# A four-layer graph network on one core: the last graph's output by halves, a closer spacing of the last graphs, and a longer hold of VectorE behind powers

## The chip, the core and the metric

One NeuronCore of a Trainium2 chip runs the whole kernel in one launch. Its engines are TensorE (PE in the profile; PEld is its weight load), VectorE (DVE), ScalarE (ACT), GpSimd (POOL) and SyncE (SP, which here issues every DMA). They run side by side and wait for each other on semaphores; each works through its own list in order. The metric is the device time of one execution in microseconds (us); lower is better.

## What is computed

There are 32 independent graphs of 512 nodes with 256 features each, all in float32. A graph passes through four layers, and each layer ends in x = layernorm(x + layer(x, adj)):

```python
# layer 0
h = (1.0 + eps) * x + adj @ x
y = relu(h @ W1 + b1) @ W2 + b2                      # 256 -> 512 -> 256
# layer 1
h = adj @ (x @ W.T + b)
y = where(h > 0, h, alpha * h)
# layer 2
h = layer_norm(x, gamma, beta)
y = x + relu((adj @ h) @ W_rel + b_rel + h @ W_root)
# layer 3
agg = eps * x + adj @ x
h = silu(rmsnorm(agg @ W1 + b1) * w)                 # 256 -> 1024
y = h @ W2 + b2                                      # 1024 -> 256
```

## The kernel before, in words

**Products.** Every large product is cut into 2 x 2 blocks and done with seven block products in place of eight (`seven`, line 648), at the price of sums of blocks on VectorE (`left_sums`, `right_sums`). A graph takes 218 matmuls, 106 with 256 columns and 112 with 128. Each leaves two records in the trace[...]. The results come out of PSUM through VectorE additions (`add` in `take` and `put`) or ScalarE copies.

**Norms.** Tokens stand on partitions: a graph's x is a tile of 128 partitions by 4 chunks by 256 features. `Norm` (line 893) gets the sum and the sum of squares of each chunk from ScalarE (`half`, two chunks at a time), scales them on VectorE, takes the power -1/2 on GpSimd (`inv_sqrt`, an instruction of 128 x 4, or of 128 x 8 in layer 1, where two scales are needed), and then scales each chunk (`scaled`, line 927) on VectorE or on ScalarE, whichever the planner finds free. The first and the last graph (`alone`, line 512) use `NormOnVector` at the end of layer 3, with `bn_stats` on VectorE in place of ScalarE's sums, and they spread the RMS norm of layer 3 over tokens with four flips by TensorE (`everywhere`, line 981, operand `ident`), where the other graphs send it through DRAM by DMA. The RMS norm of layer 3 has a power of 32 x 16.

**How the order is made.** Nothing is issued while the layers are traced. Each operation goes into a list (`Plan.do`, `Plan.move`) with the engines it may run on and a cost per engine. `order` (line 351) then plays a list schedule: at each step it takes the engine that can start first, and on it the ready operation of the lowest rank; the operations are issued in the order in which they were picked. Rank is a due time: the graph's number times `period` (42), plus the place of the operation in its graph, counted back from the matmul that needs it (`needs`, line 321). The last few graphs are spaced by `last` instead of `period`: with FLIGHT = 5 (line 496) `final` is graph 27 (line 353), and graphs 28 to 31 follow at 20 or at 12. `best` (line 345) tries each entry of RULES (line 92) as (period, pace, last, near) and keeps the one whose order ends first in the planner's own count; here it is the first entry, 20. Up to five graphs are in work at once, and the buffers (36 rooms in SBUF, 11 small tiles, 8 PSUM banks) limit what may start.

**The hold.** A GpSimd power reads SBUF next to VectorE. The planner marks VectorE operations with two tensor operands in SBUF (TWO_OPERANDS, line 79) with `port`. When VectorE has computed the input of a power, `port["vector"]` is set to the end of that operation plus PORT (line 434): until then the planner starts no two-operand operation on VectorE, but others may pass. Where VectorE would stand idle for that reason, the idle time is written out as memsets of a small tile `pause`, one for every 0.11 of the planner's time (lines 1166 to 1168).

**The trace's lines.** All compute instructions are issued from line 295 and all DMAs from line 313, so lines tell little, and tiles and shapes have to be read: `room` is any large tile, `few` a small one, `ps` a PSUM bank, `L_gnn_*` and `A` are weights and their block sums. `ps<-L_gnn_W,room` and `ps<-A,room` with 128 columns are the last products of layers 0 and 3 (`dense_add`, line 847).

Of the kernel before, what the change touches and what calls it, by code (L numbers as in the profile page):

```python
# [11 lines left out]
AF = mybir.ActivationFunctionType  # L12
ALU = mybir.AluOpType
# [3 lines left out]
LN_EPS = 1e-5  # L17
# [3 lines left out]
def span(ap):  # L21

    n = 1
    for d in ap.shape[1:]:
        n *= d
    return n
# [13 lines left out]
def vector_time(n):  # L40
    return 0.06 + n * 0.00106, 0.085
# [20 lines left out]
def power_time(n):  # L62
    return 0.3 + n * 0.18, 0.2 + 0.06 * n
# [13 lines left out]


TWO_OPERANDS = ("tensor_add", "tensor_sub", "tensor_mul", "scalar_tensor_tensor")
PORT = 0.35  # L80


SOON = 0.03
# [3 lines left out]

RULES = [(42, 2, 20, 0.5), (42, 2, 12, 0.25)]


class Pool:
# [122 lines left out]
class Plan:  # L218
# [126 lines left out]
    def best(self):  # L345


        rule = min(RULES, key=lambda rule: self.order(*rule)[0])
        return self.order(*rule)[1]

    def order(self, period, pace, last, near):

        final = max(op.graph for op in self.ops) - self.flight + 1
        rank = [
            (min(op.graph, final) * period + max(op.graph - final, 0) * last + need, i)
            for i, (op, need) in enumerate(zip(self.ops, self.needs(pace, near)))
# [14 lines left out]
        done = []  # L371
        while can_start:
# [31 lines left out]
            for i in can_start:  # L404
                op = self.ops[i]
# [17 lines left out]
            op = self.ops[i]  # L423
# [4 lines left out]
            if engine == "vector":  # L428
# [4 lines left out]
                if any(n in powers for n, _ in op.then):  # L433
                    port["vector"] = t + busy + PORT
            if op.kbytes:
# [23 lines left out]
def tile_gnn_stack(ctx: ExitStack, tc: tile.TileContext, a: dict, out: bass.AP):  # L459
# [26 lines left out]
    B, N, D = a["x"].shape  # L486
# [6 lines left out]
    HC = NC // 2  # L493
# [8 lines left out]
    plan = Plan(nc, FLIGHT)  # L502
# [9 lines left out]
    def alone():  # L512

        return plan.graph in (0, B - 1)
# [12 lines left out]
    def vector(method, n, *args, **kw):  # L527
        return "vector", method, vector_time(n), args, kw

    def scalar(func, n, x, times=scalar_time, **kw):  # L530
        columns = sum(k in ("scale", "bias") and not isinstance(v, float) for k, v in kw.items())
        return "scalar", "activation", times(n, columns), (x,), dict(func=func, **kw)

    def mm(o, lhsT, rhs, first, last):
        kw = dict(start=first, stop=last, skip_group_check=True)
        way = "tensor", "matmul", matmul_time(rhs.shape[-1]), (lhsT, rhs), kw
        plan.do(o, way, ordered=o.room)
# [4 lines left out]
    def act(o, x, func, **kw):  # L542
        plan.do(o, scalar(func, span(o), x, **kw))
# [7 lines left out]
    def add(o, x, y):  # L551
        plan.do(o, vector("tensor_add", span(o), x, y))
# [4 lines left out]
    def mul(o, x, y):  # L557
        plan.do(o, vector("tensor_mul", span(o), x, y))

    def ts(o, x, s1, s2, op0, op1=None):  # L560
        kw = dict(op0=op0) if op1 is None else dict(op0=op0, op1=op1)
        plan.do(o, vector("tensor_scalar", span(o), x, s1, s2, **kw))
# [9 lines left out]
    def inv_sqrt(o, x):  # L572
        n, p = span(o), o.shape[0]
        plan.do(
            o, ("gpsimd", "tensor_tensor", power_time(n), (x, mhalf[0:p, 0:n]), dict(op=ALU.pow))
        )


    def room(*shape):
        return Part(Room(rooms)).shaped(*shape)  # L580

    def short(*shape):
        return Part(Room(rooms, whole=False)).shaped(*shape)
# [4 lines left out]
    def bank(*shape):  # L588
        return Part(Room(banks)).shaped(*shape)

    def tok():
        return room(NC, D)

    def half(t, h):
        return t[:, h * HC : (h + 1) * HC]
# [52 lines left out]
    def seven(x, y, z, product, take, put):  # L648


        product("m1", x, True)
        take(x, 0, 0)
        product("m5", z, True)
        take(z, 1, 1)
        product("m2", y, True)
        put(y, 0, 0, True)
        product("m6", x, False)
        take(x, 0, 1)
        product("m3", z, False)
        put(z, 0, 1, True)  # L660
        product("m7", x, False)
        put(x, 1, 1, True)
        product("m4", x, False)
        put(x, 1, 0, False)
# [29 lines left out]
    def blocks_of(*halves):  # L694

        return (W[:, :, i * P : (i + 1) * P] for i in range(2) for W in halves)
# [67 lines left out]
    def aggregate(x, adjacency):  # L764

        aT = room(DC, N)
        blocks = [
            x[:, j * HC : (j + 1) * HC, k * P : (k + 1) * P] for j in range(2) for k in range(2)
        ]
        t = room(4, HC, P)  # L770
        right = right_sums(*blocks, [t[:, i] for i in range(3)], t[:, 3])

        def product(m, ps, first):
            for k in range(HC):
                mm(ps, right[m][:, k, :], adjacency.left[m][:, k, :], first and k == 0, k == HC - 1)

        def block(i, k):
            return aT[:, k, i * TH : (i + 1) * TH]

        def take(ps, i, k):  # L780
            copy(block(i, k), ps)

        def put(ps, i, k, more):
            if more:
                add(block(i, k), ps, block(i, k))
            else:
                take(ps, i, k)

        seven(*(bank(TH) for _ in range(3)), product, take, put)
        return aT  # L790
# [56 lines left out]
    def dense_add(x, right, left, done):  # L847


        def block(i, j):  # L850
            return x[:, j * HC : (j + 1) * HC, i * P : (i + 1) * P]

        def product(m, ps, first):
            n = len(right[m])
            for k in range(n):
                for i in range(HC):
                    mm(
                        ps[:, i, :], right[m][k][:, i * P : (i + 1) * P], left[m][:, k, :],
                        first and i == 0 and k == 0, k == n - 1,
                    )  # L860

        def take(ps, i, j):
            add(block(i, j), ps, block(i, j))

        def put(ps, i, j, more):
            take(ps, i, j)
            if i == 1:
                done(j)

        seven(*(bank(HC, P) for _ in range(3)), product, take, put)  # L870
# [22 lines left out]
    class Norm:  # L893
# [24 lines left out]
        def scales(self, *affine):  # L918
# [5 lines left out]
            n = len(affine) * NC  # L924
            inv_sqrt(self.rstd[:, 0:n], self.ve[:, 0:n])

        def scaled(self, i=0):

            y = self.r if i == self.last else tok()
            s, shift = (t[:, i * NC : (i + 1) * NC] for t in (self.rstd, self.shift))  # L930
            mul(shift, self.less, s)
            for c in range(NC):
                r, scale = self.r[:, c, :], s[:, c : c + 1]
                plan.do(
                    y[:, c, :],
                    vector(
                        "tensor_scalar", D, r, self.less[:, c : c + 1], scale,
                        op0=ALU.add, op1=ALU.mult,
                    ),
                    scalar(AF.Identity, D, r, scale=scale, bias=shift[:, c : c + 1]),  # L940
                )
            return y

    class NormOnVector(Norm):
# [58 lines left out]
    def plus_row(x, r):  # L1003

        for h in range(2):
            add(half(x, h), half(x, h), r.unsqueeze(1).to_broadcast([P, HC, D]))
# [13 lines left out]
    def load_x(b):  # L1020
        x = tok()
        plan.move(x, a["x"][b].rearrange("(p c) d -> p c d", c=NC), N * D / 256, late=1.6)
        return x
# [55 lines left out]
    def layer3(x, adjacency, b):  # L1079

        aT = aggregate(x, adjacency)
        plus_row(x, b2_3)
        hT, acc = Wide(FC3), short(N)

        def squares(f):
            sq = room(2, N)
            act(sq, hT.pair(f), AF.Square)
            if f == 0:
                add(acc, sq[:, 0, :], sq[:, 1, :])
            else:  # L1090
                add(acc, acc, sq[:, 0, :])
                add(acc, acc, sq[:, 1, :])

        dense_feat(aT, A1_3, b1_3, hT, squares)
        pr = everywhere(column_sums(acc), (1.0 / HID3, RMS_EPS, ALU.mult, ALU.add))
        right = {}
        for q in range(0, FH, 2):
            for f in (q, q + 1, FH + q, FH + q + 1):
                mul(hT.chunk(f), hT.chunk(f), pr)
                act(hT.chunk(f), hT.chunk(f), AF.Silu, scale=w_3[:, f : f + 1])  # L1100
            for m, t in dense_sums([hT.pair(q)], [hT.pair(FH + q)]).items():
                right[m] = right.get(m, []) + t
        norm = (NormOnVector if alone() else Norm)(x)
        dense_add(x, right, A2_3, norm.half)
        norm.scales((1.0, LN_EPS))
        y = norm.scaled()
        place = out[b].rearrange("(p c) d -> p c d", c=NC)
        plan.move(place, y, N * D / 256, into=f"out{b}")

# [7 lines left out]
    x = load_x(0)  # L1119
# [16 lines left out]
    x = layer0(x, adjacency)  # L1136
# [9 lines left out]
    h = layer1(x, adjacency)  # L1146
# [9 lines left out]
    A2_3 = weight_sums("A2_3", *blocks_of(W2_3[:, 0:FH], W2_3[:, FH:]))  # L1156
    layer3(layer2(*h, adjacency), adjacency, 0)
    for b in range(1, B):
        plan.graph = b
        x, adjacency = load_x(b), Adjacency(b)  # L1160
        h = layer1(layer0(x, adjacency), adjacency)
# [45 lines left out]
```

## Time and profile before

| | us |
|---|---|
| median of 3 runs (lowest 2336.43, highest 2342.0) | 2337.26 |
| the profiled execution, its own time | 2338.08 |
| its span, first to last instruction | 2336.3 |
| TensorE busy | 2304.8 |
| VectorE busy | 2139.5 |
| ScalarE busy | 1630.1 |
| GpSimd busy | 261.9 |

The page has, in this order: the busy time of each engine; the span in 40 slices with the busy share of each in tenths; the DMA queues; the chain of work that ended last, with its shares; the costliest groups of instructions; and the DMA issues. A group names output<-input, the partitions by elements of both, how often, busy time and mean in ns, and the idle time of its engine just before it with what ended it. Matmuls overlap each other, and a record of one lasts longer than the distance to the next, so TensorE that is "busy" may still have waited; distances between starts show it.

The mean granted clock of TensorE was 0.997 of full speed. The DMA engines were seven tenths busy in the first slice and at most two tenths in the others, and the last output of 512 KB landed 2.7 us after its issue.

### The profile page before, as it was taken

The numbers are of one execution on the slowest core, as the hardware profiler recorded it, in microseconds if no ns is written. First come the engines' busy times: TensorE is split into PE (matmuls) and PEld (weight loads), VectorE is DVE, ScalarE is ACT, GpSimd is POOL, SyncE is SP. The second block draws the span as 40 slices with busy tenths as digits, with TensorE's granted clock in tenths as the row PEclk, the third lists the DMA queues.
The fourth block names the chain that finished last, engine by engine and source line by source line (L and its number), as shares of the span: only waits on it lengthen the run. The fifth ranks groups of instructions, "written<-read, shape, count | busy, mean of one in ns | idle before, by whom it ended". The sixth has DMA issues, their size and how long they took to land.

```text
span 2336.3 us, 41057 instructions
## 1 busy us (share of the span) xinstructions
PE 2304.8 (99%) x14002; PEld 2105.4 (90%) x14002; DVE 2139.5 (92%) x5411; ACT 1630.1 (70%) x4409; POOL 261.9 (11%) x166
## 2 busy tenths in 40 slices
PE   9899999999999999999999999999999999999997
PEld 7798999999999999999999999999999999898997
DVE  8998999999999999999999999999999999899987
ACT  4676677766776776777767767767777677676775
POOL 0001101101101101011011011010110101101110
PEclk9999999999999999999999999999999999999999
DMA  7002122122221122211222211222112222121001
GB/s 239 19 19 57 24 57 54 28 56 62 57 60 28 56 57 64 55 47 37 57 62 57 60 27 56 57 63 56 44 38 58 62 60 58 23 65 55 15 17 39
DMA packets 223458, 122.83 MB, mean 53 GB/s; under 512 B 142864, under 2 KB 194320, under 8 KB 223248
## 3 DMA queue, kind: packets, MB, share of 16 engines
q1 hardware_dynamic: 223248, 120.20, 18.8%
q8 instruction: 111, 1.82, 0.3%
q14 instruction: 99, 0.81, 0.1%
HBM read 78.92 MB, written 24.97 MB: 44 GB/s over the span
## 4 chain that ended last, share of the span: by engine, by line
PE 73%; DVE 22%; issue 2%; ACT 2%; DMA 1%; POOL 0%; SPq 0%; DVEq 0%; POOLq 0%; ACTq 0%
PE ps L295 73%; DVE room L295 19%; DVE few L295 2%; ACT room L295 1%; ACT scrap L295 1%; DMA L_gnn_W<-in_L_gnn_W_dram 0%; DMA L_gnn_ln_beta_c<-in_L_gnn_ln_beta_dram 0%; POOL few L295 0%; DMA room<-in_adj_dram 0%; SPq L313 0%; DVE A L295 0%; DVEq L295 0%; POOLq L1203 0%; DVE L_gnn_W_root L295 0%; DVE pause L1168 0%
## 5 line engine op out<-in xcount | busy, mean ns | idle before, releaser
L295 PE MATMUL ps<-room,room 128*128 128x256 f32 x3584 | 920.1, 382 | 6.1 <-DVE room L295 1.9
L295 DVE TENSOR_TENSOR room<-room,room 128x512 f32<-128x512 f32 (+1 forms) x1360 | 783.4, 594 | 7.2 <-ACT room L295 4.4
L295 DVE TENSOR_TENSOR room<-ps,room 128x256 f32<-128x256 f32 (+1 forms) x1344 | 611.1, 470 | 143.3 <-PE ps L295 134.3
L295 PEld LDWEIGHTS ps<-room,room 128*128 128x128 f32 x3584 | 625.6, 191 | 73.7 <-DVE room L295 10.0
L295 PE MATMUL ps<-L_gnn_W,room 128*128 128x128 f32 (+1 forms) x3584 | 539.5, 291 | 6.5 <-ACT room L295 4.5
L295 PEld LDWEIGHTS ps<-L_gnn_W,room 128*128 128x128 f32 x3584 | 505.1, 192 | 39.2 <-ACT room L295 5.7
L295 POOL TENSOR_TENSOR few<-few,mhalf 128x4 f32<-128x4 f32 (+2 forms) x160 | 261.1, 1638 | 2068.7 <-DVE few L295 1969.4
L295 PEld LDWEIGHTS ps<-A,room 128*128 128x128 f32 x3072 | 453.5, 191 | 37.3 <-DVE room L295 3.7
L295 PE MATMUL ps<-A,room 128*128 128x128 f32 x3072 | 467.3, 275 | 1.6 <-DVE room L295 1.5
L295 PE MATMUL ps<-room,L_gnn_W 128*128 128x256 f32 x1536 | 419.8, 381 | 0.6 <-DVE room L295 0.5
L295 ACT ACTIVATE room<-room,few 128x256 f32<-128x256 f32 x590 | 316.7, 595 | 114.2 <-DVE few L295 113.1
L295 ACT ACTIVATE room<-room 128x1024 f32<-128x1024 f32 (+2 forms) x260 | 241.5, 941 | 165.2 <-DVE room L295 159.5
L295 ACT ACTIVATE room<-ps,L_gnn_b_c 128x256 f32<-128x256 f32 x768 | 309.9, 476 | 49.2 <-PE ps L295 42.2
L295 ACT ACTIVATE room<-ps 128x256 f32<-128x256 f32 (+1 forms) x515 | 180.6, 377 | 232.5 <-PE ps L295 231.5
L295 PE MATMUL ps<-room,A 128*128 128x256 f32 x1152 | 332.6, 381 | 5.5 <-ACT room L295 5.4
L295 DVE TENSOR_TENSOR room<-room 128x256 f32<-128x256 f32 (+1 forms) x640 | 312.9, 498 | 10.6 <-ACT room L295 3.0
L295 PEld LDWEIGHTS ps<-room,L_gnn_W 128*128 128x128 f32 x1536 | 276.3, 191 | 34.9 <-DVE room L295 2.5
L295 ACT ACTIVATE scrap<-room 128x256 f32<-128x256 f32 x504 | 206.7, 411 | 93.9 <-DVE room L295 84.2
L295 ACT ACTIVATE scrap<-room,few 128x256 f32<-128x256 f32 x504 | 251.9, 502 | 27.4 <-DVE few L295 25.4
L295 PEld LDWEIGHTS ps<-room,A 128*128 128x128 f32 x1152 | 198.9, 191 | 23.3 <-ACT room L295 6.7
L295 ACT ACTIVATE room<-room,L_gnn_rms_weight_c 128x512 f32<-128x512 f32 x256 | 173.6, 714 | 14.5 <-DVE room L295 14.3
L295 DVE TENSOR_TENSOR room<-room,loop 128x256 f32<-128x256 f32 x256 | 103.4, 411 | 4.1 <-PE ps L295 2.3
(57 smaller groups left out, 1131.7 us busy)
## 6 DMA issues: line engine op xcount, KB each, us to landing
room<-in_adj_dram SPq DMA_DIRECT2D x128, 256.0 KB, 5.1
room<-in_x_dram SPq DMA_DIRECT2D x32, 512.0 KB, 5.9
out_dram<-room SPq DMA_DIRECT2D x32, 512.0 KB, 3.1
room<-room SPq DMA_DIRECT2D x480, 32.0 KB, 2.0
diagonal<-room SPq DMA_DIRECT2D x62, 128.0 KB, 1.8
room<-in_adj_dram SPq DMA_DIRECT2D x124, 64.0 KB, 1.9
room<-diagonal SPq DMA_DIRECT2D x62, 128.0 KB, 2.2
room<-line SPq DMA_DIRECT2D x30, 256.0 KB, 3.2
```

Source lines behind the costliest of these rows:

```text
L295: getattr(getattr(self.nc, engine), method)(to, *(put(x) for x in args), **kw)
```

## The change

Three edits go together.

1. The last graph's output. For graphs 0 to 30 the end of layer 3 is as it was: the product with its sums, one power of 128 x 4, four chunks scaled, one DMA of 512 KB. For graph 31, `done(h)` runs when half h of the tokens has its last addition: statistics of that half, then the new `finish`: scale, a power of 128 x 2, two chunks scaled, and a DMA of 256 KB.
2. The spacing. `final` is set by the new constant LATE = 3 to graph 28, so that graphs 29 to 31 are the closely spaced ones; RULES are (42, 2, 10, 0.5) and (42, 2, 16, 0.5). The planner takes the first, as it did before.
3. The hold. PORT goes from 0.35 to 0.55.

`put` is the body of the loop in `scaled`, moved into a function of its own, without a change.

```diff
-PORT = 0.35
+PORT = 0.55
...
+LATE = 3
...
-RULES = [(42, 2, 20, 0.5), (42, 2, 12, 0.25)]
+RULES = [(42, 2, 10, 0.5), (42, 2, 16, 0.5)]
...
-        final = max(op.graph for op in self.ops) - self.flight + 1
+        final = max(op.graph for op in self.ops) - LATE
...
+        def finish(self, h, m, plus, place):
+
+            mine = slice(h * HC, (h + 1) * HC)
+            ve, rstd, shift = self.ve[:, mine], self.rstd[:, mine], self.shift[:, mine]
+            ts(ve, self.squares[:, mine], m / self.n, plus, ALU.mult, ALU.add)
+            inv_sqrt(rstd, ve)
+            mul(shift, self.less[:, mine], rstd)
+            for c in range(h * HC, (h + 1) * HC):
+                self.put(c, self.r, rstd[:, c % HC : c % HC + 1], shift[:, c % HC : c % HC + 1])
+            plan.move(place, half(self.r, h), N * D / 512, into=f"out{plan.graph}{h}")
...
-        dense_add(x, right, A2_3, norm.half)
-        norm.scales((1.0, LN_EPS))
-        y = norm.scaled()
         place = out[b].rearrange("(p c) d -> p c d", c=NC)
-        plan.move(place, y, N * D / 256, into=f"out{b}")
+        if b < B - 1:
+            dense_add(x, right, A2_3, norm.half)
+            norm.scales((1.0, LN_EPS))
+            y = norm.scaled()
+            plan.move(place, y, N * D / 256, into=f"out{b}")
+        else:
+
+            def done(h):
+                norm.half(h)
+                norm.finish(h, 1.0, LN_EPS, half(place, h))
+
+            dense_add(x, right, A2_3, done)
```

Because the whole order of issue comes out of the planner, each of the two constants changes it from the first graphs on: TensorE's order is the same up to its matmul 112, VectorE's up to its operation 94. In the built program VectorE has 65 pause memsets where it had 22, 30 scalings of chunks have gone from VectorE to ScalarE over the run, and SP's queue has one DMA more.

More of the change, by code (lines that the diff above doesn't have):

```diff
@@ L925, in scales, with put @@
             inv_sqrt(self.rstd[:, 0:n], self.ve[:, 0:n])
+        def finish(self, h, m, plus, place):
[7 more added lines that the diff above has]
+            plan.move(place, half(self.r, h), N * D / 512, into=f"out{plan.graph}{h}")
+        def put(self, c, y, scale, shift):
+            r = self.r[:, c, :]
+            plan.do(
+                y[:, c, :],
+                vector(
+                    "tensor_scalar", D, r, self.less[:, c : c + 1], scale, op0=ALU.add, op1=ALU.mult
+                ),
+                scalar(AF.Identity, D, r, scale=scale, bias=shift),
+            )
         def scaled(self, i=0):
@@ L932, in scaled @@
             for c in range(NC):
[L933 to L941, printed above, removed]
+                self.put(c, y, s[:, c : c + 1], shift[:, c : c + 1])
             return y
```

## The prediction, as put on record

> **What bounds the kernel now.** I read the page first.
>
> ```profile
> span 2336.3 us, 41057 instructions
> PE 2304.8 (99%) x14002; PEld 2105.4 (90%) x14002; DVE 2139.5 (92%) x5411; ACT 1630.1 (70%) x4409; POOL 261.9 (11%) x166
> ...
> PE   9899999999999999999999999999999999999997
> ...
> PE 73%; DVE 22%; issue 2%; ACT 2%; DMA 1%; POOL 0%; SPq 0%; DVEq 0%; POOLq 0%; ACTq 0%
> ```
>
> TensorE (PE) is the bound: a nine in every slice but the second and the last. The matmuls are the same before and after, so only time in which TensorE waits can go. The table by stage says where that is (columns: window, length, then busy time of PE, PEld, DVE, ACT, POOL, clock, DMA share, GB/s):
>
> ```profile
> 0.00:58.40 58.40, 53.55 (x264) 44.99 (x265) 50.14 (x146) 25.25 (x61) 1.73 (x7) 1.00 0.75 239
> 58.40:116.80 58.40, 51.73 (x283) 45.60 (x283) 56.39 (x155) 40.27 (x120) 5.29 (x4) 0.97 0.07 19
> ...
> 1401.60:1460.00 58.40, 58.32 (x366) 53.73 (x365) 54.67 (x135) 41.42 (x116) 8.46 (x5) 1.00 0.19 57
> ...
> 1985.60:2044.00 58.40, 56.09 (x325) 50.59 (x324) 50.22 (x128) 38.18 (x107) 7.57 (x4) 0.97 0.10 22
> ...
> 2277.60:2336.00 58.40, 45.54 (x329) 43.00 (x327) 43.13 (x103) 33.20 (x78) 4.62 (x5) 0.92 0.11 41
> ```
>
> A busy matmul still hides short waits, so I also took starts from the timeline of TensorE: unhindered, a record follows the one before after 0.111 us (128 columns) or 0.218 us (256), and two records make a matmul. What exceeds that, summed: 16.6 us in 0-120; 3.0 in 180-300; 10.7 in 300-1980; 6.5 in 1980-2160; nothing in 2160-2280; 7.7 from 2280 to the last matmul's end at 2328.2. After it come 8.1 us without a matmul. In the steady stretch each graph is alike: 218 matmuls in 71.5 us, 0.5 of them lost.
>
> The last 7.7 us, in the timeline:
>
> ```profile
> 2306.29 2.05 PE L295 MATMUL ps<-L_gnn_W,room 128*128 128x128 f32 x16 [0.52 <-DVE room L295]
> ...
> 2310.13 0.65 PE L295 MATMUL ps<-ident,few 128*128 128x128 f32 x4 [1.79 <-POOL few L295]
> 2313.01 7.25 PE L295 MATMUL ps<-L_gnn_W,room 128*128 128x128 f32 x48 [2.23 <-ACT room L295]
> 2320.10 5.52 PE L295 MATMUL ps<-A,room 128*128 128x128 f32 x48
> 2326.14 2.05 PE L295 MATMUL ps<-L_gnn_W,room 128*128 128x128 f32 x16 [0.52 <-DVE room L295]
> ```
>
> The flips (`ident`) of graph 31's RMS norm wait for its power, the last product for the silu behind it, and no other graph has matmuls left: graph 30's ended just before the flips. By starts these four waits cost 0.68 + 1.95 + 2.39 + 0.68 = 5.7 us.
>
> **What the Trainium skill says.** "Perfetto Trace Analysis", section "Identifying the Most-Contended Engine": a matmul's busy share is no measure of headroom. The trace agrees: 99% busy, yet the starts show 44 us lost between matmuls, where the page's idle 31.5, less 9.3 at the two ends, is 22. "GPSIMD Engine Reference", section "8. Key points": GpSimd shares its SBUF interfaces with VectorE and contends with instructions of two SBUF inputs. The trace agrees:
>
> ```profile
> L295 POOL TENSOR_TENSOR few<-few,mhalf 128x8 f32<-128x8 f32 x32 | 72.9, 2278 | 383.9 <-DVE few L295 351.5 <-ACT room L295 32.4
> ...
> L295 DVE TENSOR_SCALAR room<-room,few 128x256 f32<-128x256 f32 x50 | 19.4, 409 | 0.0
> ...
> L1168 DVE MEMSET pause<- 128x48 f32 x22 | 2.2, 98 | 1.1
> ```
>
> The power of 128x8 takes 1.64 us where it is undisturbed (at 311.2), 2.28 in the mean, and at 382.7, where a two-operand add starts 0.07 us after it, it and the next power take 3.56 where 1.64 + 1.01 would do. VectorE's own adds there keep their 0.41 us.
>
> **The change part by part.** I read the list in which each built program issues its work over all engines and added up, between neighbouring matmuls, the VectorE and ScalarE work priced with trace rows. Before, the largest stand at matmul 251 (4.3 VectorE, 4.3 ScalarE; trace: 5.3 lost), 633 (1.9, 2.3; 1.46 lost), 6111 and 6113 (1.6 and 1.4; 1.15 and 1.47 lost), the last flips (2.2; 1.95) and what follows them (2.5; 2.39). So the count finds the long waits.
>
> Start (0-120): the matmul order is the same up to number 112, and at 251 the count is 4.3 and 4.3 again: 0, at most 1 either way.
>
> Hold of 0.55 (PORT), graphs 1 to 4: the 1.46 us at 633 (graph 1's final product) have no successor; smaller ones (1.5 of the 3.0) may stay. -1.5.
>
> Hold, steady graphs (22): per graph one two-operand multiply now stands behind one pause memset (0.10 us busy, 65 memsets in all against 22), and one scaling of 128x256 goes from VectorE (0.34 from start to start) to ScalarE (0.52; it works 48 of 71.5 us). VectorE work per graph 63.7 to 63.3 us, TensorE 71.0 on the same matmuls. Behind a pausing VectorE stand the additions that empty PSUM and the sums that TensorE reads; what hides the pause is VectorE's idle time, 4.6 us per graph, 2.7 of it in one wait for TensorE. Without that cover it costs 22 x 0.1 = 2. The 0.5 us lost per graph are VectorE running late over a stretch without idle time; I see no reason for a sign and take 0. Bounds: all of it goes, -11; it becomes 0.9, the worst of the 22 now, +9.
>
> Spacing 20 to 10, over three graphs rather than four: the waits at 2032-2157 (1.15 + 1.47 + 0.36 + 0.49 = 3.5) go with the order that made them. After matmul 251 the new order has two places over 1.3 us: matmul 6323 (ScalarE 1.67, less 0.43 for the matmul: 1.2) and 6695 (1.37: 0.9). At the end, graph 31's flips now have ten matmuls of graphs 29 and 30 behind them and its final product mixes with graph 30's until 28 matmuls before the end, where it was alone for 56. Ten times 0.22 = 2.2 us cover the multiply and silu (0.68 + 0.71 and hand-overs: 2.9 from flip to matmul before). The four waits of 5.7 go. Of the other 5.0 in 1980-2328 (14.2 - 3.5 - 5.7) I keep half. Sum: -14.2 + 2.1 + 2.5 = -9.6.
>
> Halves for the last graph: its first half is scaled and sent while the second is computed. Before, from the last matmul's end: addition and statistics 1.95, power 1.01, multiply and two scalings per engine to 4.28, issue to landing 2.69 (first packet 0.82 after issue, 512 KB in 1.45), then 1.1 to the end: 8.1. After: two small VectorE instructions more (0.3), a power of 128x2 (below 1.01, above 0: I take 0.7), one scaling per engine (-0.5), 256 KB (-0.7). That alone would be about -1. But the closer spacing leaves graphs 29 and 30 unfinished: in the last 9.1 us of matmuls ScalarE has 8 scalings at 0.52 and 12 sums at 0.42 to 0.51 queued, so graph 30's last sum ends about 1.6 after the last matmul; on VectorE graph 30's scale stands ahead of graph 31's second statistics, on GpSimd its power (1.01) ahead of the last one, on ScalarE three of its scalings (1.6) ahead of graph 31's, on SP's queue its 512 KB ahead of the last 256. The last scaling ends near 5.4 instead of 4.28, the landing near 8.4 after the matmul instead of 7.0. The DMA page ("DMA: Bandwidth & Descriptors", section "Specifications") gives 0.6 us to the first byte from the sync path; the trace's 0.82 is used. +1.2 (from +0.2 to +1.8).
>
> Sum: -1.5 + 0 - 9.6 + 1.2 = -9.9. The profiled execution took 2338.08 (span 2336.3 and 1.8 around it), so 2328.2; it lies 0.8 above the median of 2337.26, so I put the median at 2327.5.
>
> **The rivals.** *Better steady graphs:* powers that start undisturbed let VectorE run on time, and the 0.5 per graph falls below 0.25. For it: the disturbed 128x8 power now has only small, PSUM and one-operand work in its first 0.7 us. Against: VectorE was not seen idle for it. -5.5 to -11: 2316.5 to 2322.
>
> *The gain is handed back:* the loss per graph grows to 0.7-0.9 (+4 to +9), or the ramp-down keeps its small waits and the tail's queue costs 1.8. 2331 to 2337.
>
> *Slower, VectorE waits for the power:* in the new order the two multiplies of layer 1's scalings follow their power's input by only 3.0 us of other VectorE work (3.35 in the trace before). VectorE is in order, so if the power is not back, everything behind the multiplies waits, the PSUM additions first, then TensorE. The power needs 0.17 + 1.64 undisturbed or 2.55 disturbed (3.56 less 1.01); from 2.8 on it decides, and slower than now by 0.3% needs (2344.3 - 2327.5) / 22 = 0.76 us per graph, a power of 3.6. The pair's 3.56 shows that such lengths exist; the 0.7 us of harmless work put before the first two-operand one speaks against. About 2346.
>
> That the change does nothing is excluded for the tail, since the order differs.
>
> **How the numbers follow.** Forecast (2323.5 to 2331.5 with its own bounds) 0.60, better steady graphs 0.16, handed back 0.16, slower 0.08. Under 0.3%, 7 us, a measurement can't tell from no change: faster is below 2330.25, slower above 2344.3. Nine tenths of the forecast and all of the second case are faster: 0.70; the rest of the forecast and the third are the same: 0.22; slower 0.08. The range 2319 to 2335 leaves out half of the second case, a quarter of the third and the fourth: 0.20.
>
> **What would show it.** Right: the last slice with about 5 us more of TensorE, no wait over 1 us from 2280 to the last matmul, that matmul's end near 2317, and 9 to 9.5 us after it; steady graphs of 71.5 us; no wait at 232. Wrong: graphs of over 71.8 or under 71.2 us, a VectorE wait for GpSimd in each graph, a ramp-down from 1980 that loses over 5 us, or ScalarE not the one that ends last.

## The result and the profile after

The changed kernel took 2323.3 us (median of 4 runs, 2321.73 to 2325.38) where the kernel before took 2339.61 beside it (4 runs): ratio 0.9932, 95% interval 0.992 to 0.9944. It is 16 us faster, and the forecast of 2327.5 was 4 us too high. The profiled execution of the changed kernel took 2325.38, the longest of its four.

The page of the changed kernel, the lines that answer to those shown of before:

```profile
span 2323.6 us, 41135 instructions
PE 2298.6 (99%) x14002; PEld 2096.4 (90%) x14002; DVE 2121.5 (91%) x5426; ACT 1639.9 (71%) x4439; POOL 256.4 (11%) x167
...
PE   8899999999999999999999999999999999999998
...
PE 90%; DVE 6%; ACT 1%; DMA 1%; issue 1%; SPq 0%; POOL 0%; ACTq 0%; DVEq 0%
```

TensorE is still the bound. The share of VectorE on the chain that ended last went from 22% to 6%. That share is no measure of the time lost: it is 13% with a hold of 0.45 below, which is slower than the kernel before. The same stages in the table by stage (window, length, then busy time of PE, PEld, DVE, ACT, POOL, clock, DMA share, GB/s), of the changed kernel:

```profile
58.09:116.18 58.09, 51.60 (x275) 44.52 (x275) 54.76 (x150) 37.69 (x114) 5.29 (x4) 0.94 0.07 19
1394.16:1452.25 58.09, 58.09 (x366) 53.26 (x365) 52.59 (x127) 41.51 (x117) 4.91 (x3) 1.00 0.20 56
1974.00:2032.00 58.00, 57.80 (x363) 53.13 (x362) 54.47 (x141) 40.03 (x113) 5.88 (x4) 1.00 0.26 85
2265.50:2323.60 58.10, 48.93 (x396) 47.38 (x394) 44.07 (x109) 38.75 (x96) 5.36 (x6) 0.96 0.12 42
```

The second slice has the same hole as before. The steady slice, where TensorE was busy 58.32 of 58.40 us, is full. The slice near 1990 has 1.7 us more of TensorE, the last one 3.4 more. The end of TensorE's timeline in the changed kernel:

```profile
2307.75 4.63 PE L298 MATMUL ps<-A,room 128*128 128x128 f32 x40
2312.89 2.05 PE L298 MATMUL ps<-L_gnn_W,room 128*128 128x128 f32 x16 [0.52 <-DVE room L298]
```

Three of the four waits of the old tail are gone. The fourth, for the addition that empties the accumulating bank before the last product, stands where it stood, 0.68 us by starts. The prediction's own count said that graph 31's last 28 matmuls stand alone, so nothing was there to cover this one.

The ramp-down and the tail before held something more than waits, which the clock shows (same columns; the kernel before, then the changed one):

```profile
2036.80:2040.22 3.42, 3.42 (x12) 2.94 (x11) 3.14 (x8) 3.42 (x8) 1.18 (x1) 0.50 0.02 3
2313.28:2316.70 3.42, 3.42 (x18) 3.42 (x18) 3.42 (x7) 2.92 (x6) 0.00 (x0) 0.50 0.00 0
...
114.00:2319.00 2205.00, 2197.66 (x13495) 2010.20 (x13494) 2020.09 (x5140) 1579.67 (x4272) 249.37 (x156) 1.00 0.18 49
```

Behind the waits near 2033 and 2311 the granted clock was half of full speed for 3.4 us. The matmuls there, at twice their usual distance, lost 1.7 and 1.6 us. In the changed kernel, where those waits are gone, the clock stays full from 114 us on.

Where all of it went is read from the starts, as in the prediction: what the distances exceed 0.111 us (128 columns) or 0.2175 (256) per record. (With the prediction's rounded 0.218 every entry of the steady column is 2.3 lower; the differences between kernels stay.) The sums are cut here at the same matmul numbers in every kernel: 0 to 300 is the start, 300 to 900 graphs 1 to 4, 900 to 5696 the 22 steady graphs, 5696 to 7013 the ramp-down and the tail; "end" is from the end of the last matmul to the end of the span. A span is 2280.85 us plus these five numbers. Each row is one profiled execution, in us:

| kernel | start | graphs 1-4 | steady | of it per graph | ramp-down, tail | end | sum |
|---|---|---|---|---|---|---|---|
| before | 16.9 | 3.3 | 12.6 | 0.57 | 14.6 | 8.1 | 55.5 |
| changed | 21.2 | 2.1 | 4.8 | 0.22 | 6.0 | 8.65 | 42.8 |
| changed, a second execution | 18.2 | 2.1 | 5.0 | 0.23 | 6.6 | 8.6 | 40.6 |
| hold alone | 19.1 | 2.1 | 4.9 | 0.22 | 13.6 | 8.1 | 47.7 |
| spacing alone | 18.7 | 3.3 | 11.7 | 0.53 | 7.6 | 9.4 | 50.6 |
| halves alone | 17.3 | 3.2 | 11.7 | 0.53 | 13.1 | 7.1 | 52.4 |
| changed, hold back at 0.35 | 19.4 | 3.2 | 11.7 | 0.53 | 7.4 | 9.7 | 51.5 |
| changed, final norm whole | 18.8 | 2.1 | 4.9 | 0.22 | 6.4 | 8.8 | 41.0 |
| changed, no memsets | 21.9 | 2.1 | 5.1 | 0.23 | 4.8 | 8.7 | 42.7 |
| changed, hold 0.8 | 12.1 | 5.6 | 13.3 | 0.60 | 6.2 | 7.6 | 44.8 |
| changed, hold 0.45 | 17.9 | 16.1 | 17.6 | 0.80 | 11.4 | 9.6 | 72.5 |
| changed, hold 0.45, no memsets | 16.7 | 15.0 | 9.7 | 0.44 | 11.9 | 9.5 | 62.8 |
| hold 0.8 early, then 0.55, no memsets | 11.8 | 5.0 | 5.4 | 0.24 | 4.9 | 8.7 | 35.8 |

The steady column is where the forecast missed: it had 0 there, and 7.8 us went.

### The profile page after: what moved, and what is told of

It is laid out like the page before. It is cut to its first block, busy times and chain, and to the rows that moved or that the text cites. A ratio compares the mean times of both kernels' runs of the same rounds, so it can differ in the third digit from the quotient of the medians.

```text
span 2323.6 us, 41135 instructions
## 1 busy us (share of the span) xinstructions
PE 2298.6 (99%) x14002; PEld 2096.4 (90%) x14002; DVE 2121.5 (91%) x5426; ACT 1639.9 (71%) x4439; POOL 256.4 (11%) x167
## 3 DMA queue, kind: packets, MB, share of 16 engines
q1 hardware_dynamic: 223392, 120.20, 19.1%
## 4 chain that ended last, share of the span: by engine, by line
PE 90%; DVE 6%; ACT 1%; DMA 1%; issue 1%; SPq 0%; POOL 0%; ACTq 0%; DVEq 0%
PE ps L298 90%; DVE room L298 5%; ACT room L298 1%; ACT scrap L298 1%; DVE few L298 1%; DMA room<-in_x_dram 0%; DMA L_gnn_W<-in_L_gnn_W_dram 0%; DMA L_gnn_eps<-in_L_gnn_eps_dram 0%; DMA room<-room 0%; SPq L316 0%; DVE A L298 0%; DVE L_gnn_W L298 0%; POOL few L298 0%; DVE pause L1192 0%; ACTq L1227 0%
## 5 line engine op out<-in xcount | busy, mean ns | idle before, releaser
L298 PE MATMUL ps<-room,room 128*128 128x256 f32 x3584 | 933.5, 383 | 6.4 <-DVE room L298 3.3
L298 DVE TENSOR_TENSOR room<-room,room 128x512 f32<-128x512 f32 (+1 forms) x1360 | 773.1, 590 | 2.2 <-ACT room L298 0.3
L298 PEld LDWEIGHTS ps<-A,room 128*128 128x128 f32 x3072 | 459.9, 191 | 47.1 <-DVE room L298 14.4
L298 PE MATMUL ps<-A,room 128*128 128x128 f32 x3072 | 486.1, 276 | 1.1 <-DVE room L298 0.9
L298 POOL TENSOR_TENSOR few<-few,mhalf 128x4 f32<-128x4 f32 (+2 forms) x161 | 255.7, 1595 | 2061.0 <-DVE few L298 1879.2
L298 ACT ACTIVATE room<-room,few 128x256 f32<-128x256 f32 x620 | 331.6, 596 | 151.8 <-DVE few L298 148.4
L298 PE MATMUL ps<-room,A 128*128 128x256 f32 x1152 | 320.4, 381 | 5.5 <-ACT room L298 5.5
L298 ACT ACTIVATE room<-ps 128x256 f32<-128x256 f32 x515 | 180.7, 372 | 163.3 <-PE ps L298 163.0
```

Source lines behind the costliest of these rows:

```text
L298: getattr(getattr(self.nc, engine), method)(to, *(put(x) for x in args), **kw)
```

## The experiments

The theory after the result: each edit acts in a stage of its own. The hold gives the steady graphs, the spacing the ramp-down and the tail, the halves 1 us at the end, most of which the closer spacing takes back. The rival: the steady graphs were better by chance, and all of the gain is in the ramp-down and the tail.

**The hold alone.**

```diff
-PORT = 0.35
+PORT = 0.55
```

> The kernel before with the hold of 0.55 alone (spacing and final norm as before). Theory (the gain of the steady graphs comes from the hold): TensorE loses about 0.2 us per steady graph instead of 0.5, period 71.2 us, -7.5 in all; the waits before matmul 900 lose about 1 less; the four waits of the tail stay (5.7 us), 8.1 us after the last matmul. Together 8 to 9 us below the kernel before. Rival (the steady graphs were better by chance of one execution, all of the gain is in the ramp-down and the tail): within 2 us of the kernel before, steady period 71.5.

Measured: 2330.3 us beside 2338.42 before, ratio 0.9962 (0.9948 to 0.9976), 8.1 below. In the table the steady graphs lose what they lose in the changed kernel, and the tail keeps its waits. The rival falls.

**The spacing alone.**

```diff
+LATE = 3
...
-RULES = [(42, 2, 20, 0.5), (42, 2, 12, 0.25)]
+RULES = [(42, 2, 10, 0.5), (42, 2, 16, 0.5)]
...
-        final = max(op.graph for op in self.ops) - self.flight + 1
+        final = max(op.graph for op in self.ops) - LATE
```

> The kernel before with the spacing of 10 over three graphs alone (hold 0.35, final norm whole). Theory: steady graphs as before (0.5 us lost each, 71.5 us), ramp-down and tail lose 6 to 7 us instead of 14.6, and the end after the last matmul grows from 8.1 to about 9.7, since graphs 29 and 30 are still queued and the last graph is not halved: 6 to 7 us below the kernel before. Rival (all of the gain is here): 12 to 13 us below.

Measured: 2333.22, ratio 0.998 (0.9972 to 0.9988), 5.2 below. The ramp-down and tail lose 7.0 less, the end grows by 1.3, the steady graphs stay within 1 us: as the theory said, a little less of it.

**The halves alone**: the changed kernel with the hold and the spacing put back (the other two diffs reversed).

> The kernel before with the last graph's final norm by halves alone (hold 0.35, spacing 20 over four graphs). TensorE's order is that of the kernel before. Theory: nothing changes between matmuls, and the time after the last matmul falls from 8.1 to about 7 us, because no other graph is queued there: 1 us below the kernel before, which is hardly to be told from nothing. Rival (the halves cost, by two more small VectorE instructions, a second power and a second transfer behind the first): 0.5 to 1 us above.

Measured: 2337.08, ratio 0.9993 (0.9985 to 1.0001). The interval doesn't tell it from no change, but the profile does: 7.1 us after the last matmul where there were 8.1. The three parts alone add up to 8.1 + 5.2 + 1.3 = 14.6 us below; the changed kernel was 16.3 below in its first runs and 14.8 in the later ones.

**The changed kernel with the old hold.**

```diff
-PORT = 0.55
+PORT = 0.35
```

> The changed kernel with the hold back at 0.35 (spacing and halves as changed). Theory: steady graphs lose 0.5 us again, the wait of 1.5 us at matmul 633 is back, the tail has no wait over 1 us: 8 us above the changed kernel, 5 us or so below the kernel before once the loading start, which varies by some us from run to run, is taken out (7 to 8 below). Rival (all of the gain is in the ramp-down and the tail): as the changed kernel, within 2 us.

Measured: 2333.92, ratio 0.9977 (0.9969 to 0.9985), 4.5 below the kernel before. The steady 0.53 us per graph are back, for the theory. It is some 2 us slower than spacing and halves alone would add up to, and the table places 1.3 of that at the end, which is 9.7 instead of 9.4 less the 1.0 of the halves. So the parts don't add up: without the hold the halves gain nothing at the end (9.7 with them, 9.4 without).

**How the hold works: the memsets left out.** The hold could work in two ways. Either the powers run undisturbed and their results are in time (theory B), or the hold only makes the planner put other work first (theory A). Here the order of every engine is that of the changed kernel, and the memsets that keep VectorE waiting are not issued.

```diff
-                for _ in range(round(op.pause / 0.11)):
+                for _ in range(0):
```

> The changed kernel with its order on every engine as it is, but without the memsets that hold VectorE off the powers. Theory A (the hold works as an order: the planner puts additions that empty PSUM ahead of the two-operand work behind a power, and TensorE's stalls at the two places of each graph go): steady graphs lose 0.2 us or less as in the changed kernel, though the powers are stretched, and the time is that of the changed kernel or up to 1 us less. Theory B (the hold works by powers that run undisturbed, so that their results and VectorE's work behind them are on time): 0.4 to 0.5 us lost per graph, 5 to 7 us above the changed kernel.

Measured: 2322.46, ratio 0.9932 (0.992 to 0.9945), the changed kernel's own. The steady loss is 0.23. So the memsets themselves give nothing.

This run alone doesn't exclude theory B: the 128x8 power takes 2.28 us in the mean of the kernel before, 1.64 in the changed kernel, and 1.64 without the memsets too. What excludes B is that the steady time doesn't follow the powers' lengths. The groups of GpSimd (shape, count, busy time, mean ns), of the changed kernel:

```profile
L298 POOL TENSOR_TENSOR few<-few,mhalf 128x4 f32<-128x4 f32 x97 | 116.3, 1200 | 736.9 <-DVE few L298 658.3 <-DVE pause L1192 48.9 <-ACT scrap L298 29.7
...
L298 POOL TENSOR_TENSOR few<-few,mhalf 128x8 f32<-128x8 f32 x32 | 52.3, 1636 | 348.9 <-DVE few L298 303.4 <-DVE pause L1192 29.3 <-ACT room L298 16.3
```

The same of the kernel with a hold of 0.8, whose powers are the shorter ones and whose steady graphs lose three times as much:

```profile
L298 POOL TENSOR_TENSOR few<-few,mhalf 128x4 f32<-128x4 f32 x97 | 100.7, 1045 | 740.3 <-DVE few L298 667.7 <-DVE pause L1192 43.5 <-ACT scrap L298 29.1
...
L298 POOL TENSOR_TENSOR few<-few,mhalf 128x8 f32<-128x8 f32 x32 | 52.4, 1636 | 356.3 <-DVE few L298 337.4 <-DVE pause L1192 18.9
```

The 128x8 power is as short with 0.8 as in the changed kernel. The 128x4 power even got longer in the changed kernel, 1.20 us where it was 1.04 before and is 1.05 with 0.8. The memsets don't make the difference between the two kernels either: the steady graphs have 22 of them in one and 21 in the other.

What the order does can be seen by folding the steady stretch at 218 matmuls. In the kernel before, the same few matmuls are late in every graph: two neighbours by 0.26 and 0.10 us, where layer 2's aggregate of one graph begins, and two by 0.14 and 0.07, where layer 0's first dense product of another begins; two smaller ones of 0.08 and 0.05 stand elsewhere. The second place, in the timeline of the kernel before:

```profile
958.58 0.42 DVE L295 TENSOR_TENSOR room<-room,room 128x256 f32<-128x256 f32 x1
...
958.91 0.42 DVE L295 TENSOR_TENSOR room<-ps,room 128x256 f32<-128x256 f32 x1
959.11 0.38 PE L295 MATMUL ps<-A,room 128*128 128x128 f32 x2
...
959.48 0.45 PE L295 MATMUL ps<-room,L_gnn_W 128*128 128x256 f32 x1
```

The matmul at 959.48 should have started at 959.33. Its operand comes out of the VectorE addition of a PSUM bank (`room<-ps,room`, 958.91 to 959.33), and that stood behind the two-operand sums of another graph (the last of three at 958.58). In the changed kernel the issue list has the same addition ahead of those three. Its timeline:

```profile
956.60 0.40 DVE L298 TENSOR_TENSOR room<-ps,room 128x256 f32<-128x256 f32 x1
...
959.86 0.38 PE L298 MATMUL ps<-room,L_gnn_W 128*128 128x256 f32 x1
```

The addition is done 2.9 us before that graph's product at 959.86, and TensorE doesn't wait for it. The first place, before and then changed:

```profile
923.37 0.83 PE L295 MATMUL ps<-L_gnn_W_root,room 128*128 128x128 f32 x6
923.82 0.40 DVE L295 TENSOR_TENSOR room<-ps,room 128x256 f32<-128x256 f32 x1
924.28 0.91 PE L295 MATMUL ps<-room,room 128*128 128x256 f32 x3
...
923.82 1.05 PE L298 MATMUL ps<-L_gnn_W_root,room 128*128 128x128 f32 x8
924.26 0.73 DVE L298 TENSOR_TENSOR room<-ps,room 128x256 f32<-128x256 f32 x2
924.72 1.13 PE L298 MATMUL ps<-room,room 128*128 128x256 f32 x4
```

Here the new list has four products (8 records) of the dense layer ahead of the aggregate where three (6) stood, 0.22 us more cover for an addition that comes no sooner; 0.10 us of the loss stays. At both places VectorE's instructions last as long as before.

So the hold acts through the planner. At the second place it is what its rule says: work with two operands in SBUF may not start for a while, and an addition out of PSUM, which may, is picked first. At the first place it is a change of TensorE's own order that came with it. Together the two places lose 0.45 us less per graph. The new order has late places of its own: two neighbours among the products with `A` lose 0.20 where they lost 0.04.

One rival goes with the order: in each steady graph one scaling has moved from VectorE to ScalarE, and VectorE's busy time per graph fell from 66.0 to 65.4 us. No run moves it alone. The kernel before tells what it was worth there:

```profile
896.84 0.41 DVE L295 TENSOR_SCALAR room<-room,few 128x256 f32<-128x256 f32 x1
897.84 1.23 DVE L295 TENSOR_TENSOR room<-ps,room 128x512 f32<-128x512 f32 x2 [0.59 <-PE ps L295]
```

Right behind the scaling VectorE was idle for 0.59 us, waiting for TensorE, and for 2.7 us once more at 905.5. So the scaling didn't make the additions at 924 and 959 late. And with a hold of 0.45, without memsets, it has moved too, while 0.44 us per graph stay lost.

**A hold of 0.8 and of 0.45.** If it is the order, a longer hold need not be better.

```diff
-PORT = 0.55
+PORT = 0.8
```

> The changed kernel with the hold at 0.8: another order, 92 memsets. Theory A (order): the order at the first of the two places is as at 0.55; the loss does not follow the hold's length: steady graphs lose 0.1 to 0.4 us, within 4 us of the changed kernel on either side. Theory B (undisturbed powers): shorter powers, a loss below 0.2 per graph, 1 to 4 us below the changed kernel.

Measured: 2328.38, ratio 0.9958 (0.9944 to 0.9971), 5 us above the changed kernel, where A allowed 4 and B wanted less than the changed kernel. A's size was wrong too: the steady graphs lose 0.60 us each, where it had 0.1 to 0.4. B has the wrong direction, and falls.

```diff
-PORT = 0.55
+PORT = 0.45
```

> The changed kernel with the hold at 0.45: another order on VectorE, and 165 memsets where 65 were. Theory A (order): at the first of the two places (the addition of graph 12's weights product ahead of the right sums) the order is as at 0.55 but for one memset, so that stall is gone; the loss per steady graph is 0.2 to 0.35, the additional memsets costing at most 100 x 0.1 = 10 us if VectorE had no idle time, and I expect 0 to 3: 0 to 4 us above the changed kernel. Theory B (undisturbed powers): between 0.35 and 0.55, about 4 us above the changed kernel, with powers of 128x8 between 1.64 and 2.28 us.

Measured: 2355.72, ratio 1.0073 (1.006 to 1.0086): slower than the kernel before, and 32 us above the changed kernel. Both theories had at most about 4, so both sizes were wrong. A value between 0.35 and 0.55 gave the worst order of all: graphs 1 to 4 lose 16 us and the steady graphs 0.80 each. The largest wait of graphs 1 to 4, in TensorE's timeline of this kernel:

```profile
206.71 1.03 PE L298 MATMUL ps<-room,A 128*128 128x256 f32 x4
211.76 1.65 PE L298 MATMUL ps<-room,L_gnn_W 128*128 128x256 f32 x3 [4.03 <-DVE room L298]
```

It has 165 memsets too, about five in each steady graph, so order and memsets were still mixed. The same kernel without them (the diff of the memsets again):

> The kernel with the hold at 0.45, same order on every engine, without its 165 memsets. It was 32 us above the changed kernel with them. Theory A (the order makes the loss): no more than 5 us below the kernel with its memsets (2351 to 2356 beside a kernel before of 2338), the waits of 4 us early on and the loss per steady graph stay. Rival (the memsets, some 5 in each steady graph, make VectorE late): back to 2324 to 2335.

Measured: 2344.74, ratio 1.0026 (1.0016 to 1.0036). Neither range held, 2351 to 2356 or 2324 to 2335: 11 us were the memsets, 21 the order. In the steady graphs 112 memsets cost 17.6 - 9.7 = 7.9 us, 0.07 each of their 0.10. The changed kernel has one for each steady graph, and leaving it out gained nothing there (0.22 and 0.23). So the cover that the prediction named, VectorE's idle time, hides one but not five.

**The final norm whole again.**

```diff
-        if b < B - 1:
+        if b < B:
```

> The changed kernel with the last graph's final norm whole. TensorE's order is the same. In the first four experiments the halves took 1 us off the end alone (8.1 to 7.15), but with the closer spacing and the hold of 0.35 the end was 9.7 with them and 9.4 without. Theory (the queue of graphs 29 and 30 on ScalarE sets the end, so halving gains nothing there): within 0.5 us of the changed kernel, the end after the last matmul between 8.4 and 9.0. Rival (halves still shorten the last transfer and scaling): 1 us above the changed kernel, the end 9.6.

Measured: 2323.63, ratio 0.9935 (0.9923 to 0.9948), the changed kernel's time; the end is 8.8 us where it is 8.65. With the closer spacing, the halves give 0.2 of the 1.0 us that they give alone. Why shows in the timeline of the changed kernel after its last matmul, which ends at 2314.95:

```profile
2315.97 1.09 ACT L298 ACTIVATE room<-room,few 128x256 f32<-128x256 f32 x2
2316.03 0.17 DVE L298 TENSOR_SCALAR few<-few 128x4 f32<-128x4 f32 x1
...
2316.28 1.67 POOL L298 TENSOR_TENSOR few<-few,mhalf 128x4 f32<-128x4 f32 x2 [1.24 <-DVE few L298]
...
2317.32 0.16 DVE L298 TENSOR_TENSOR few<-few 128x4 f32<-128x4 f32 x1 [0.24 <-POOL few L298]
2317.58 1.09 ACT L298 ACTIVATE room<-room,few 128x256 f32<-128x256 f32 x2 [0.53 <-DVE few L298]
```

Graph 30's scale (128x4, 2316.03) waits for ScalarE's last sum at 2316.00; its power (1.0 us) runs ahead of graph 31's second one (0.7); and ScalarE, with four scalings left, waits for it until 2317.58.

**An order from two holds.** The hold of 0.8 lost only 12.1 us in the first 300 matmuls, since its order has no wait of over 5 us near matmul 250, and so no stretch of half clock behind it. The prediction's count of work between neighbouring matmuls finds this too: 4.3 us of VectorE and 4.3 of ScalarE work there in the changed kernel, at most 0.8 and 1.5 at 0.8. So the two were put together, without the memsets:

```diff
+EARLY = 0.8
+UNTIL = 260
...
-                    port["vector"] = t + busy + PORT
+                    port["vector"] = t + busy + (EARLY if t < UNTIL else PORT)
...
-                for _ in range(round(op.pause / 0.11)):
+                for _ in range(0):
```

> The changed kernel with a hold of 0.8 in the planner's first 260 us (graphs 0 to 3) and 0.55 after it, and without the memsets: an order made from the early part of the kernel with the hold of 0.8 and the rest of the changed kernel. If the parts go by order alone: 12 to 14 us lost in matmuls 0 to 300 (the wait of 5.6 us near matmul 250 is gone, as with 0.8), 4.5 to 5.5 in 300 to 900, and from there on the losses of the changed kernel (4.8 in the steady graphs). That is 2 to 5 us below the changed kernel: 2318 to 2321 beside a kernel before of 2338. If the early waits are given back where the two orders meet: as the changed kernel, 2323.

Measured: 2318.04 (2317.81 to 2318.36), ratio 0.9912 (0.9898 to 0.9925), 5.9 below the changed kernel beside it (2323.96), a little more than expected. It beats both kernels, and each stage of it loses what the same order lost elsewhere: 11.8 at the start (12.1 at a hold of 0.8), 5.0 (5.6) in graphs 1 to 4, 0.24 (0.22) per steady graph.

**The changed kernel once more**, for the start, which had cost 4.3 us more than before in the first profiles.

> The changed kernel once more, for a second profiled execution. From matmul 300 on, the losses should be those of the first within 0.3 us in each stretch; before it they were 16.9 to 21.9 us in seven executions of kernels with the same or nearly the same early order, so 17 to 22 is expected, and the number of matmuls that take 0.86 us instead of 0.43 after the first waits should account for the difference.

Measured: 2323.96, ratio 0.9938 (0.9925 to 0.9952). From matmul 300 to 900 it agrees within 0.1 us with the first execution, in the steady graphs within 0.2, in the ramp-down only within 0.6. The start lost 18.2 instead of 21.2. The first execution, around the long wait of the start:

```profile
108.04 2.08 PE L298 MATMUL ps<-room,A 128*128 128x256 f32 x4 [5.46 <-ACT room L298]
...
110.76 1.92 PE L298 MATMUL ps<-room,L_gnn_W 128*128 128x256 f32 x4
```

and the second:

```profile
106.46 2.07 PE L298 MATMUL ps<-room,A 128*128 128x256 f32 x4 [5.46 <-ACT room L298]
...
109.17 1.25 PE L298 MATMUL ps<-room,L_gnn_W 128*128 128x256 f32 x4
```

The wait is the same, but the group of four records at `L_gnn_W` took 1.92 us in one and 1.25 in the other, where four normally take 1.03. The granted clock was half from 107.2 to 114.0 us in the first and from 106.2 to 109.6 in the second. The slow matmuls behind that wait make 1.4 of the 3.0 us. Another 1.5 come from a stretch of half clock in the loading, 11.6 to 15.0 us, which the second doesn't have there; 0.5 more is one wait in the loading (1.70 and 1.20), and 0.4 goes the other way. The Trainium skill, "TensorE: Matmul & The Clock Gate", section "Part 1: The HAM clock gate", says that an idle window of about 3.4 us halves the clock, that the window runs free of the kernel, and that the number of slow matmuls so varies from run to run. The trace agrees on the rate, 0.427 us against 0.218, and on the variation, with stretches of 3.4 and 6.8 us. It doesn't need that long a wait: in the kernel before, waits of 1.15 and 1.47 us close together were enough, near 2033.

## Why the prediction was right, and where it was not

| step | forecast | first execution | second |
|---|---|---|---|
| start | 0, at most 1 either way | +4.3 | +1.3 |
| hold, graphs 1 to 4 | -1.5 | -1.2 | -1.2 |
| hold, steady graphs | 0 (-11 to +9) | -7.8 | -7.6 |
| spacing, ramp-down and tail | -9.6 | -8.6 | -8.0 |
| after the last matmul | +1.2 (+0.2 to +1.8) | +0.5 | +0.5 |
| sum | -9.9 | -12.7 | -14.9 |

The sign, the range and three of the five steps held, and the closeness of the sum is in part luck: in the first execution the start's +4.3 hides over half of the steady -7.8. The start, the other step that missed, is taken up below. The term that was mis-sized is the steady one: "The 0.5 us lost per graph are VectorE running late over a stretch without idle time; I see no reason for a sign and take 0." It measured -7.8. What the step took as a diffuse lateness was a handful of fixed places, and at the two largest the late addition could be named. Folding the trace at 218 matmuls would have shown them before any change was run, and the issue list of the changed program would have shown there what is ahead of it. The rival "better steady graphs" had the right size of this term (-5.5 to -11) for a wrong reason: it spoke of undisturbed powers, and with a hold of 0.8 the powers are undisturbed while 0.60 us per graph stay lost.

*Hold, early graphs:* the wait of 1.46 us at matmul 633 went, as said, and is back with the old hold (3.2 against 2.1 us).

*Spacing:* the four waits were to go; three did, and 0.68 stayed. Of the two new waits that the count gave, 1.2 at matmul 6323 came as 1.30 one matmul earlier; 0.9 at 6695 didn't come, the nearest being 0.57 at 6716. The hold has a share in this stage: with the old one it loses 7.4 instead of 6.0. What the prediction called "the other 5.0" and halved without a reason was for 3.3 us the two stretches of half clock; its own table has the clock below full in both slices, 0.97 and 0.92. They went with the waits before them.

*After the last matmul:* alone the halves gain 1.0, as "about -1" said. The queue of graphs 29 and 30 was the right mechanism, and was put 0.7 us too long: ScalarE's last sum ended 1.0 us after the last matmul where 1.6 was counted, and its last scaling 4.7 where 5.4 was. The power of 128x2 took 0.70 us, as taken.

*Start:* the bound of 1 us was too narrow. The two orders differ little there (the wait near matmul 250 is 5.6 instead of 5.3), but executions of one kernel differ by 3 us, mostly by how long the half clock lasts, and the forecast had no term for that.

*What would show it:* no wait over 1 us from 2280 on, none at 232, and ScalarE ending last, right. The last slice was to have 5 us more of TensorE and has 3.4, the last matmul was to end near 2317 and ended at 2314.95, with 8.65 us after it instead of 9 to 9.5. Two signs of being wrong came up: graphs of 71.5 us took 71.20, at the edge that was named, and the ramp-down from 1980 loses 5.4 us with the prediction's distances (5.9 with the table's), over the 5 that were named.

*Slower, VectorE waits for the power:* no such wait appeared in the steady graphs. A slower outcome was near all the same: a hold of 0.45 gives one, by its order and its memsets.

## What to carry to other kernels

Where a planner or a list makes the order, judge a constant by the order that comes out and not by what the constant is named for: here a guard for GpSimd's powers won 8 us through the order, where an addition out of PSUM passed other sums and where TensorE got one more product as cover. Fold a periodic trace at its period before calling a loss diffuse, and name the late instruction at each place. And don't expect such a constant to act smoothly: 0.35, 0.45, 0.55 and 0.8 gave 0.53, 0.80, 0.22 and 0.60 us lost per graph.

## What the runs showed of the hardware

The half rate of TensorE after waits, and its varying length (3.4 or 6.8 us), make most of the 3 us by which the start varies with one order; the rest repeats to some tenths. It needs no single long wait: waits of 1.52 and 1.72 us, 2.2 us apart, brought it with a hold of 0.45 (from 166.4 us on), and waits of 1.50 and 1.70, 3.9 us apart, didn't with 0.8 (near 155). One wait of 2.5 us (2.49 and 2.54) brought it in the run of 0.45 without memsets and not in the run with them. Such a stretch cost 1.5 to 1.8 us where it was 3.4 us long, and 2.0 to 3.1 where it was 6.8, on top of the waits before it. GpSimd's power over 128 x 8 takes 1.64 us when no two-operand VectorE work meets it and 2.28 in the mean of the kernel before. The Trainium skill ("GPSIMD Engine Reference", section "8. Key points") tells of that contention, and the trace agrees; none of the 8 us came from its end. A pause memset of 0.10 us on VectorE cost 0.07 us of the whole where five stand in a graph, and nothing where there is one. Why a hold of 0.8 removes the long wait of the start was followed no further than the count of work there, and why it loses more in the steady graphs no further than its powers and memsets.
